# A^T h of a four-layer graph network in 64x64 parts of the TensorE array

## The chip, the cores and the metric

The kernel runs on one core of one Trainium2 chip. The metric is the device time of one execution in microseconds (us), lower is better. A core has TensorE (PE in the profile; its weight loads are listed apart as PEld), VectorE (DVE), ScalarE (ACT), GpSimd (POOL) and the engine that issues transfers (SP). Each engine takes its instructions from a queue of its own, in the order in which the program put them there. Matmuls write to PSUM, which has eight banks of 2 KB per partition; the other data live in SBUF.

## What is computed

128 graphs of 64 nodes with 256 features pass through four layers, each with a layer norm, a ReLU and a residual: attention with four heads, attention with one head, a relational layer, and a gated graph network with three GRU steps. The change concerns the last one:

```python
def _gru_cell(inp, h, w_ih, w_hh, b_ih, b_hh):
    gi = inp @ w_ih.T + b_ih
    gh = h @ w_hh.T + b_hh
    i_r, i_z, i_n = jnp.split(gi, 3, axis=-1)
    h_r, h_z, h_n = jnp.split(gh, 3, axis=-1)
    r = jax.nn.sigmoid(i_r + h_r)
    z = jax.nn.sigmoid(i_z + h_z)
    n = jnp.tanh(i_n + r * h_n)
    return (1.0 - z) * n + z * h

def _L3_gnn_ref(x, adj, weight, w_ih, w_hh, b_ih, b_hh):
    A = (adj != 0).astype(x.dtype)
    h = x
    for i in range(3):
        m = jnp.einsum('bnd,de->bne', h, weight[i])
        aggr = jnp.einsum('bst,bsd->btd', A, m)
        h = _gru_cell(aggr, h, w_ih, w_hh, b_ih, b_hh)
    return h

# each layer:
h = jnp.maximum(_layernorm(x, axis=-1), 0.0)
x = x + layer(h, adj, ...)
```

All data are fp32. The kernel uses A^T (h W) = (A^T h) W: it forms A^T h and multiplies it with the combined weights `wc` (weight[i] times w_ih).

## The kernel before

Two graphs lie side by side on the 128 partitions and make a pair; four pairs (G = 4, eight graphs, T = 512 columns) make a group, and there are 16 groups. The 256 features are two chunks of 128 (K = 2). The state h is kept with features on the partitions (`hT`) and, for A^T h, with nodes on the partitions (`hnat`); `abd` holds the adjacency as 0 and 1.

`along` forms one chunk c of A^T h for a group. A graph has only 64 nodes, so a product sums over 64 partitions. The two graphs of a pair stand on the two halves of the partitions, and their products use the two halves of the array's rows at the same time; each has 64x128 weights (`hnat`) and streams the 64 columns of `abd`. `beside` enters such a set of products into the plan as one operation of the given cost.

```python
def beside(products, cost):
    def emit():
        for product in products:
            nc.nc.tensor.matmul(*[real(x) for x in product], start=True, stop=True)
    ...
    nc.note("PE", emit, cost, ...)

def along(psum, hnat, abd, aT, c):
    pa, pb = psum.tile([P, G, N], F32, name="tp"), psum.tile([P, G, N], F32, name="tq")
    products = []
    for p in range(G):
        for half, ps in ((0, pa), (1, pb)):
            b = slice(half * N, (half + 1) * N)
            products.append((ps[:, p, :], hnat[b, p, c * P : (c + 1) * P], abd[b, p, :]))
    beside(products, 700.0)
    to = aT[:, c, :].rearrange("p (g a j) -> p a g j", a=2, j=N)
    nc.scalar.copy(to[:, 0], pa)
    nc.scalar.copy(to[:, 1], pb)
```

It is called for both chunks ahead of the recurrence, and for each chunk in steps 1 and 2 of the recurrence; step 0 takes the A^T h formed ahead of it.

```python
def before_recurrence(work, psum, src, adjacency, abd, by_dma=False):
    ... # layer norm: hT and hnat; abd
    for c in range(K):
        along(psum, hnat, abd, aT, c)
    ... # sums of parts of hT and aT

# recurrence, step i (gate, mul, both: matmuls with 128x128 weights):
a.gate("nh", 0)
if i > 0:
    aT = work.tile([P, K, T], F32, name="aT")
    along(psum, hnat, abd, aT, 0)
    state_sums(aT, aS, 0)
a.mul("ry", 1, 1)
a.m1_there()
a.gate("ni", 0)
if i > 0:
    back(hT, hnat, 1)          # transposes chunk 1 of the state into hnat
a.gate("nh", 1)
a.nh_there()
if i > 0:
    along(psum, hnat, abd, aT, 1)
    state_sums(aT, aS, 1)
...
```

The attention layers have a set in 64x64 parts already. The rows of the array are halved by r, its output columns by a, and each r has a PSUM bank of its own (`mm`, `mn`):

```python
for h in range(heads):
    for a in range(2):
        for r in range(2):
            b, s, to = slice(r * N, (r + 1) * N), 2 * u + a, slice(a * N, (a + 1) * N)
            products.append((pv[r][to, h, :], t[b, s * heads + h, :], wv[b, s, h, :]))
beside(products, 800.0 if heads > 1 else 600.0)
```

The program isn't emitted in the order in which it is written. A plan notes every operation with an estimated cost in ns, its dependencies and a stretch of time (a job with start and end), from which it gets a due time; it then simulates the engines and emits, on each engine, the operation that can start first, by due time among equals. `LATENCY` is what the simulation adds between an operation and its user on another engine. So costs, latency and stretches decide only the order in each queue. The recurrence of a group runs while the first three layers of later groups fill the gaps.

```python
LATENCY = 176.7
...
nc.begin("weights", 18.0, 84.9)
...
start, period = 94.8, 82.2
...
at = start + g * period
nc.begin(("before", g), at - (13.0 if g == 0 else 17.8), at, ...)
before(g)
nc.begin(("recur", g), at, at + period)
recur(g)
```

Of the kernel before, what the change touches and what calls it, by code (L numbers as in the profile page):

```python
# [8 lines left out]
F32 = mybir.dt.float32  # L9
# [7 lines left out]
P = 128  # L17
N = 64
D = 256
K = D // P  # L20
G = 4
# [115 lines left out]
class Pool:  # L137
# [3 lines left out]
    psum = False  # L141
# [66 lines left out]
class Plan:  # L208

    LATENCY = 176.7

    def __init__(self, nc):
        self.nc, self.on, self.ops, self.job = nc, False, [], None
# [221 lines left out]
def kernel(  # L437
# [28 lines left out]
    nc = Plan(tc.nc)  # L466
# [128 lines left out]
# [8 lines that stand above are left out]
        if not nc.on:  # L603
            return emit()
        writes = list({id(x[0].base): x[0] for x in products}.values())
        nc.note("PE", emit, cost, [Plan.all_of(x) for x in writes], [x for p in products for x in p[1:]])
# [57 lines left out]
    def aggregate_graphs(work, psum, t, wv, heads):  # L664


        fo = D // heads
        n = wv.shape[1]
        o = work.tile([P, n, heads, fo], F32, name="o")
        for u in range(n // 2):  # L670
            banks = [psum.tile([P, 512], F32, name=name) for name in ("mm", "mn")]
            pv = [po[:, : D + heads].rearrange("p (h f) -> p h f", h=heads) for po in banks]
# [3 lines that stand above are left out]
                    for r in range(2):  # L676
                        b, s, to = slice(r * N, (r + 1) * N), 2 * u + a, slice(a * N, (a + 1) * N)
                        products.append((pv[r][to, h, :], t[b, s * heads + h, :], wv[b, s, h, :]))
            beside(products, 800.0 if heads > 1 else 600.0)
            for r in range(2):  # L680
                rec = work.tile([P, heads], F32, name="rec")
                nc.vector.reciprocal(rec, pv[r][:, :, fo])
                nc.vector.tensor_tensor(
                    o[:, 2 * u + r], pv[r][:, :, :fo], rec[:, :, None].to_broadcast([P, heads, fo]), ALU.mult
                )
        return o.rearrange("p g h f -> p g (h f)")

    def along(psum, hnat, abd, aT, c):

        pa, pb = psum.tile([P, G, N], F32, name="tp"), psum.tile([P, G, N], F32, name="tq")  # L690
        products = []
        for p in range(G):
            for half, ps in ((0, pa), (1, pb)):
                b = slice(half * N, (half + 1) * N)
                products.append((ps[:, p, :], hnat[b, p, c * P : (c + 1) * P], abd[b, p, :]))
        beside(products, 700.0)
        to = aT[:, c, :].rearrange("p (g a j) -> p a g j", a=2, j=N)
        nc.scalar.copy(to[:, 0], pa)
        nc.scalar.copy(to[:, 1], pb)
        return 0.9  # L700

# [23 lines left out]
    def before_recurrence(work, psum, src, adjacency, abd, by_dma=False):  # L727

        hT = work.tile([P, K, T], F32, name="hT")
        hnat = work.tile([P, G, D], F32, name="hnat")  # L730
        if by_dma:
            layernorm_T_by_dma(work, src, hT, hnat)
        else:
            layernorm_T(work, psum, src, hT, natural=hnat)
        nc.vector.tensor_scalar(abd, adjacency, 0.0, None, op0=ALU.not_equal)
        aT = work.tile([P, K, T], F32, name="aT")
        for c in range(K):
            along(psum, hnat, abd, aT, c)
        hS = work.tile([P, 4, T // 2], F32, name="hS")
        aS = work.tile([P, 4, T // 2], F32, name="aS")  # L740
        for k in range(K):
            state_sums(hT, hS, k)
            state_sums(aT, aS, k)
        return hT, aT, hS, aS

    def recurrence(work, psum, start, src, abd, store):

        hT, aT, hS, aS = start
# [102 lines left out]
        for i in range(LAYERS):  # L851
            last = i == LAYERS - 1
            hnew = work.tile([P, K, T], F32, name="hT")
            a = Chunk(0, i, hT, hnew)

            a.mul("ry", 1, 0)
            a.gate("nh", 0)
            if i > 0:
                aT = work.tile([P, K, T], F32, name="aT")
                along(psum, hnat, abd, aT, 0)  # L860
                state_sums(aT, aS, 0)
            a.mul("ry", 1, 1)
            a.m1_there()
            a.gate("ni", 0)
            if i > 0:
                back(hT, hnat, 1)
            a.gate("nh", 1)
            a.nh_there()
            if i > 0:
                along(psum, hnat, abd, aT, 1)  # L870
                state_sums(aT, aS, 1)
            a.mul("rm", 2, 0) + a.mul("rz", 7, 0)
            a.mul("rm", 2, 1)
            a.r_there(S0)
            a.mul("rz", 7, 1)
            a.gate("ni", 1)
            a.n_there(S0)
            a.both("ry", 6)
            a.m16_there()
            b = Chunk(1, i, hT, hnew)  # L880
            b.both("rm", 2)
            a.both("ry", 5)
            a.m165_there()
            a.z_there(S1)
            b.gate("nh", 0)
            a.both("ry", 3)
            a.r_there(S1)
            a.n_there(S1)
            a.h_there(S1)
            a.both("rz", 4)  # L890
            a.z_there(S0)
            a.h_there(S0)

            b.gate("nh", 1)
            b.nh_there()
            b.both("ry", 1)
            b.m1_there()
            b.r_there(S0)
            b.both("rz", 7)
            b.both("ry", 6)  # L900
            b.m16_there()
            b.gate("ni", 0)
            b.both("ry", 5)
            b.m165_there()
            b.z_there(S1)
            hnat = work.tile([P, G, D], F32, name="hnat")
            back(hnew, hnat, 0, src if last else None)
            b.both("ry", 3)
            b.r_there(S1)
            b.gate("ni", 1)  # L910
            b.n_there(S0)
            b.n_there(S1)
            b.h_there(S1)
            b.both("rz", 4)
            b.z_there(S0)
            b.h_there(S0)
            hT = hnew
            if not last:
                for k in range(K):
                    state_sums(hT, hS, k)  # L920
# [5 lines left out]
    with ExitStack() as s1:  # L926
# [34 lines left out]
        psum = Banks(s1.enter_context(tc.tile_pool(name="psum", bufs=1, space=PSUM)), 1, Banks.own)  # L961
# [203 lines left out]
        def loop_relation(g, p0, n, pool):  # L1165

            src = XG[g][:, p0 : p0 + n]
            hT = pool.tile([P, K, n * P], F32, name="hT")
# [16 lines left out]
            products = []  # L1185
            for u in range(n // 2):
                for a in range(2):
                    for r in range(2):
                        b, s = slice(r * N, (r + 1) * N), 2 * u + a
                        products.append((po[r][a * N : (a + 1) * N, u, :], oh[b, s, :], v[b, s, :]))  # L1190
            beside(products, 1050.0 * n / 4)
            for r in range(2):
                to = src.rearrange("p (u r) d -> p r u d", r=2)[:, r]
                nc.vector.scalar_tensor_tensor(to, po[r], 0.0, to, op0=ALU.max, op1=ALU.add)
# [34 lines left out]

        nc.begin("columns")  # L1230
        first_weights()
        nc.begin("weights", 18.0, 84.9)
        later_weights(early)
        layers = (first_layer, second_layer, third_layer)
        start, period = 94.8, 82.2
        users = {}
        for g in range(NG):
            if g > 1:
                load_group(g)

            if g == 0:
                units = [(0, 2, (-3.0, 30.1, 57.3, 72.2)), (2, 2, (4.1, 32.9, 59.6, 78.0))]
            elif g == 1:
                units = [(0, 2, (28.7, 55.8, 87.9, 107.3)), (2, 2, (46.0, 70.1, 100.9, 126.4))]
            elif g == 2:
                units = [(0, G, (74.9, 112.9, 175.1, 237.8))]
            else:
                end = start + g * period - 28.8
                units = [(0, G, [end - 52.1 * i for i in (3, 2, 1, 0)])]
            for p0, n, at in units:  # L1250
                spare = g == 0 and p0 > 0
                for i in range(3):
                    nc.begin((g, p0, i), at[i], at[i + 1], [users[i]] if i in users and not spare else [])
                    if not spare:
                        users[i] = (g, p0, i)
                    layers[i](g, p0, n, spare)
            if g == 0:
                nc.begin("make")
                nc.note("-", make_gru, 0.0, [], [], [op for op in nc.ops if any(b.pool is early for b in op.bases)])
            at = start + g * period  # L1260
            nc.begin(("before", g), at - (13.0 if g == 0 else 17.8), at, [("recur", g - 2)] if g > 1 else [])
            before(g)
            nc.begin(("recur", g), at, at + period)
            recur(g)
# [240 lines left out]
```

## Time and profile before

| | before |
|---|---|
| device time, median of 3 (us) | 1477.09 (1475.32 to 1477.32) |
| profiled span (us) | 1473.8 |
| granted TensorE clock, mean | 0.991 |
| sets of A^T h | 96, each of 8 products, 16 records |
| weight load of A^T h, median (ns) | 188 |
| weight load of attention, 64x64, median (ns) | 133 |
| copy of A^T h out of PSUM, 128x256, median (ns) | 372 |

In the groups of instructions, `tp<-abd,hnat 64*128 64x64 f32` is a matmul that writes the tile `tp` and reads `abd` and `hnat`, with weights of 64 rows and 128 columns, and an output as long as 64 columns. The duration of one record holds the passage through the array, and records overlap; what an operation costs the queue is read from the starts of successive records. An fp32 product is two records.

### The profile page before, as it was taken

Reading aid. Unit: us, or ns where it says so; the run is one execution under the profiler, and the core shown is the slowest. Engines: PE = TensorE matmul, PEld = TensorE weight load, DVE = VectorE, ACT = ScalarE, POOL = GpSimd, SP = SyncE. Lnnn points to the kernel's source line nnn. Section 1 sums busy time; section 2 is a strip of 40 time slices with the busy share of each in tenths; the row PEclk is TensorE's granted clock in tenths of the full one; section 3 lists DMA queues with packets and bytes.
Section 4 is the critical chain, followed back from the end, with each engine's and each line's share of the span. In section 5 each row is a group of like instructions: output and inputs, shape, how many; then the busy total and the mean of one; then the engine's idle time right before and its main releaser. Section 6 shows DMA issues by size and latency. Waiting matters only on the chain.

```text
span 1473.8 us, 24378 instructions
## 1 busy us (share of the span) xinstructions
PE 1428.2 (97%) x7925; PEld 981.2 (67%) x7925; DVE 1034.8 (70%) x2743; ACT 783.8 (53%) x1885; POOL 597.3 (41%) x744
## 2 busy tenths in 40 slices
PE   4989999999999999999999999999999999999996
PEld 3556776767667676766767676676767667666764
DVE  6678486785857778586776858577786968765543
ACT  3655556455555645555555555555555565544543
POOL 2424433444534444452434344344434434352432
PEclk8999999999999999999999999999999999999998
DMA  7011122212222121222212222221212122110000
GB/s 207 18 27 28 31 59 37 69 28 41 61 50 63 33 59 40 44 62 49 64 31 51 49 46 62 45 68 26 45 38 45 44 42 57 23 32 16 15 15 18
DMA packets 298863, 67.67 MB, mean 46 GB/s; under 512 B 274664, under 2 KB 296936, under 8 KB 298728
## 3 DMA queue, kind: packets, MB, share of 16 engines
q1 hardware_dynamic: 298168, 65.50, 21.3%
q8 instruction: 66, 1.08, 0.3%
q10 hardware_dynamic: 560, 0.52, 0.2%
q14 instruction: 69, 0.57, 0.1%
HBM read 28.06 MB, written 8.53 MB: 25 GB/s over the span
## 4 chain that ended last, share of the span: by engine, by line
PE 90%; DVE 5%; DMA 1%; SPq 1%; ACT 1%; issue 1%; POOL 0%; DVEq 0%
PE ry L380 22%; PE mm L380 15%; PE rz L380 11%; PE nh L380 11%; PE ni L380 11%; PE tp L601 6%; PE rm L380 6%; PE tp L380 4%; PE mm L601 3%; SPq L380 1%; DVE t L380 1%; DVE st L380 1%; DVE d L380 1%; DMA ihn<-in_L_gnn_w_ih_dram 1%; DMA hhn<-in_L_gnn_w_hh_dram 1%
## 5 line engine op out<-in xcount | busy, mean ns | idle before, releaser
L380 POOL TENSOR_TENSOR d<-hT,t 128x256 f32<-128x256 f32 x192 | 145.1, 763 | 492.9 <-ACT t L380 492.4
L380 PE MATMUL ni<-aT,wc 128*128 128x512 f32 x384 | 198.0, 599 | 0.2
L380 PE MATMUL nh<-hT,whh 128*128 128x512 f32 x384 | 194.7, 596 | 0.0
L380 DVE SCALAR_TENSOR_TENSOR t<-r,t 128x256 f32<-128x256 f32 x192 | 111.3, 583 | 62.6 <-ACT r L380 53.7
L380 ACT ACTIVATE z<-z,brz 128x256 f32<-128x256 f32 x192 | 97.0, 505 | 101.4 <-DVE z L380 100.9
L380 ACT COPY z<-ry 128x256 f32<-128x256 f32 x192 | 70.9, 369 | 134.3 <-PE ry L380 100.0
L380 POOL TENSOR_TENSOR hS<-hT 128x256 f32<-128x256 f32 x96 | 74.8, 783 | 136.0 <-PE ry L380 97.1
L380 DVE SCALAR_TENSOR_TENSOR d<-z,d 128x256 f32<-128x256 f32 x192 | 102.8, 545 | 36.7 <-POOL d L380 22.9
L601 PEld LDWEIGHTS tp<-abd,hnat 64*128 64x128 f32 x768 | 92.6, 187 | 48.8 <-issue 11.0
L380 PE MATMUL rz<-hS,whh 128*128 128x256 f32 x384 | 117.7, 388 | 2.4 <-DVE z L380 2.4
L380 ACT ACTIVATE hn<-xg,var,rstd 128x256 f32<-128x256 f32 x200 | 107.5, 594 | 20.4 <-DVE var L380 19.3
L380 PE MATMUL ry<-hS,wsum 128*128 128x256 f32 x384 | 116.7, 386 | 0.9 <-ACT z L380 0.8
L380 PE MATMUL mm<-wl,hT 128*128 128x512 f32 x248 | 116.2, 598 | 0.0
L380 PE MATMUL ry<-aS,wsum 128*128 128x256 f32 x384 | 114.2, 379 | 0.0
L380 PE MATMUL rz<-aS,wc 128*128 128x256 f32 x384 | 114.2, 379 | 0.0
L380 DVE TENSOR_TENSOR z<-rz,z 128x256 f32<-128x256 f32 x192 | 80.3, 418 | 47.5 <-PE rz L380 27.6
L380 ACT ACTIVATE t<-t,bi 128x256 f32<-128x256 f32 x192 | 94.9, 503 | 31.9 <-DVE t L380 30.9
L601 PE MATMUL tp<-abd,hnat 64*128 64x64 f32 x768 | 105.8, 278 | 0.0
L601 PE MATMUL tq<-abd,hnat 64*128 64x64 f32 x768 | 105.8, 278 | 0.0
L380 PEld LDWEIGHTS ry<-hS,wsum 128*128 128x128 f32 x384 | 70.1, 190 | 46.8 <-issue 24.8
L380 DVE SCALAR_TENSOR_TENSOR hT<-d,t 128x256 f32<-128x256 f32 x192 | 95.4, 510 | 4.2 <-DVE d L380 0.5
L380 POOL TENSOR_TENSOR aS<-aT,aS 128x256 f32<-128x256 f32 x96 | 75.9, 791 | 54.9 <-ACT aT L380 54.9
(200 smaller groups left out, 3270.2 us busy)
## 6 DMA issues: line engine op xcount, KB each, us to landing
hT<-hn SPq DMA_DIRECT2D x896, 32.0 KB, 1.9
out_dram<-hnat SPq DMA_DIRECT2D x16, 512.0 KB, 3.4
xg<-in_x_dram SPq DMA_DIRECT2D x15, 512.0 KB, 4.8
t<-row SPq DMA_DIRECT2D x28, 256.0 KB, 4.2
at<-in_adj_dram SPq DMA_DIRECT2D x64, 32.0 KB, 2.2
eg<-in_adj_dram SPq DMA_DIRECT2D x64, 32.0 KB, 2.2
ag<-in_adj_dram SPq DMA_DIRECT2D x16, 128.0 KB, 2.4
t<-row SPq DMA_DIRECT2D x28, 64.0 KB, 2.8
```

What stands on the lines that cost most here:

```text
L380: return do(*[real(a) for a in args], **{k: real(v) for k, v in kwargs.items()})
L601: nc.nc.tensor.matmul(*[real(x) for x in product], start=True, stop=True)
```

## The change

Three things are changed.

1. `along` now forms its products in 64x64 parts: the 128 features of a chunk are split in two halves f, which go to the two halves of the array's columns. With the two graphs of a pair on the two halves of its rows, four products can stand side by side. There are twice as many products, each with 64x64 weights.
2. `along` takes a list of chunks. Ahead of the recurrence both chunks are formed in one set, with one PSUM bank for each row half and one copy out of each bank. Within the recurrence the chunks stay apart; a branch for merging them there is switched off (`if 0`).
3. The plan's costs of the sets, its latency and its stretches are given new values. That changes the order in the queues, and no operation.

The first two are for less time of TensorE on A^T h; the third is for an order that fits.

```diff
-    LATENCY = 176.7
+    LATENCY = 160.9
@@ aggregate_graphs
-            beside(products, 800.0 if heads > 1 else 600.0)
+            beside(products, 710.0 if heads > 1 else 660.0)
@@
-    def along(psum, hnat, abd, aT, c):
-
-        pa, pb = psum.tile([P, G, N], F32, name="tp"), psum.tile([P, G, N], F32, name="tq")
+    def along(psum, hnat, abd, aT, cs):
+
+        banks = [psum.tile([P, len(cs), G, N], F32, name=name) for name in ("tp", "tq")]
         products = []
-        for p in range(G):
-            for half, ps in ((0, pa), (1, pb)):
-                b = slice(half * N, (half + 1) * N)
-                products.append((ps[:, p, :], hnat[b, p, c * P : (c + 1) * P], abd[b, p, :]))
-        beside(products, 700.0)
-        to = aT[:, c, :].rearrange("p (g a j) -> p a g j", a=2, j=N)
-        nc.scalar.copy(to[:, 0], pa)
-        nc.scalar.copy(to[:, 1], pb)
+        for i, c in enumerate(cs):
+            for p in range(G):
+                for half, ps in enumerate(banks):
+                    b = slice(half * N, (half + 1) * N)
+                    for f in range(0, P, N):
+                        products.append((ps[f : f + N, i, p, :], hnat[b, p, c * P + f : c * P + f + N], abd[b, p, :]))
+        beside(products, 230.0 + 480.0 * len(cs))
+        to = aT[:, cs[0] : cs[-1] + 1, :].rearrange("p c (g a j) -> p a c g j", a=2, j=N)
+        for half, ps in enumerate(banks):
+            nc.scalar.copy(to[:, half], ps)
@@ before_recurrence
-        for c in range(K):
-            along(psum, hnat, abd, aT, c)
+        along(psum, hnat, abd, aT, range(K))
@@ recurrence
-                along(psum, hnat, abd, aT, 0)
+                if 0:
+                    back(hT, hnat, 1)
+                    along(psum, hnat, abd, aT, range(K))
+                else:
+                    along(psum, hnat, abd, aT, [0])
...
-                along(psum, hnat, abd, aT, 1)
+                if not 0:
+                    along(psum, hnat, abd, aT, [1])
@@ loop_relation
-            beside(products, 1050.0 * n / 4)
+            beside(products, 230.0 + 216.0 * n)
@@ the plan's stretches
-        nc.begin("weights", 18.0, 84.9)
+        nc.begin("weights", 18.0, 79.1)
-        start, period = 94.8, 82.2
+        start, period = 99.2, 83.2
-                units = [(0, 2, (-3.0, 30.1, 57.3, 72.2)), (2, 2, (4.1, 32.9, 59.6, 78.0))]
+                units = [(0, 2, (0.2, 24.7, 61.4, 71.1)), (2, 2, (-0.6, 32.2, 60.6, 75.0))]
... # the units of groups 1 and 2 likewise
-                end = start + g * period - 28.8
-                units = [(0, G, [end - 52.1 * i for i in (3, 2, 1, 0)])]
+                end = start + g * period - 26.2
+                units = [(0, G, [end - 55.6 * i for i in (3, 2, 1, 0)])]
-            nc.begin(("before", g), at - (13.0 if g == 0 else 17.8), at, ...)
+            nc.begin(("before", g), at - (13.0 if g == 0 else 21.2), at, ...)
```

More of the change, by code (lines that the diff above doesn't have):

```diff
@@ L686, in aggregate_graphs @@
         return o.rearrange("p g h f -> p g (h f)")
-    def along(psum, hnat, abd, aT, c):
-        pa, pb = psum.tile([P, G, N], F32, name="tp"), psum.tile([P, G, N], F32, name="tq")
+    def along(psum, hnat, abd, aT, cs):
+        banks = [psum.tile([P, len(cs), G, N], F32, name=name) for name in ("tp", "tq")]
         products = []
-        for p in range(G):
-            for half, ps in ((0, pa), (1, pb)):
-                b = slice(half * N, (half + 1) * N)
-                products.append((ps[:, p, :], hnat[b, p, c * P : (c + 1) * P], abd[b, p, :]))
-        beside(products, 700.0)
-        to = aT[:, c, :].rearrange("p (g a j) -> p a g j", a=2, j=N)
-        nc.scalar.copy(to[:, 0], pa)
-        nc.scalar.copy(to[:, 1], pb)
-        return 0.9
+        for i, c in enumerate(cs):
[8 more added lines that the diff above has]
+            nc.scalar.copy(to[:, half], ps)
     def weight_sums(w, ws):
@@ L864, in recurrence @@
             a.gate("ni", 0)
-            if i > 0:
+            if i > 0 and not 0:
                 back(hT, hnat, 1)
@@ L1241 @@
             if g == 0:
-                units = [(0, 2, (-3.0, 30.1, 57.3, 72.2)), (2, 2, (4.1, 32.9, 59.6, 78.0))]
+                units = [(0, 2, (0.2, 24.7, 61.4, 71.1)), (2, 2, (-0.6, 32.2, 60.6, 75.0))]
             elif g == 1:
-                units = [(0, 2, (28.7, 55.8, 87.9, 107.3)), (2, 2, (46.0, 70.1, 100.9, 126.4))]
+                units = [(0, 2, (27.2, 56.6, 87.4, 98.1)), (2, 2, (44.7, 71.4, 101.8, 129.4))]
             elif g == 2:
-                units = [(0, G, (74.9, 112.9, 175.1, 237.8))]
+                units = [(0, G, (72.8, 120.6, 177.5, 238.7))]
             else:
-                end = start + g * period - 28.8
-                units = [(0, G, [end - 52.1 * i for i in (3, 2, 1, 0)])]
+                end = start + g * period - 26.2
+                units = [(0, G, [end - 55.6 * i for i in (3, 2, 1, 0)])]
             for p0, n, at in units:
@@ L1260 @@
             at = start + g * period
-            nc.begin(("before", g), at - (13.0 if g == 0 else 17.8), at, [("recur", g - 2)] if g > 1 else [])
+            nc.begin(("before", g), at - (13.0 if g == 0 else 21.2), at, [("recur", g - 2)] if g > 1 else [])
             before(g)
```

## The prediction

> **What bounds the kernel now.** I first read the page's busy times.
>
> ```profile
> span 1473.8 us, 24378 instructions
> PE 1428.2 (97%) x7925; PEld 981.2 (67%) x7925; DVE 1034.8 (70%) x2743; ACT 783.8 (53%) x1885; POOL 597.3 (41%) x744
> ```
>
> TensorE (PE) is busy 97% of the span and the next engine 70%. A busy PE can still be badly used, because matmuls are pipelined, so I asked next for the busy time by stretches, to see where the missing 3% lies.
>
> ```profile
> 0.00:100.00 100.00, 74.67 (x422) 46.49 (x422) 68.85 (x228) 51.23 (x137) 33.13 (x55) 0.91 0.35 90
> ...
> 800.00:1000.00 200.00, 198.92 (x1143) 137.72 (x1142) 146.71 (x393) 109.37 (x262) 82.19 (x100) 1.00 0.25 54
> 1400.00:1474.00 74.00, 60.66 (x280) 41.41 (x278) 29.32 (x66) 29.56 (x68) 20.91 (x28) 0.94 0.05 16
> ```
>
> The columns after the length are PE, weight loads, DVE, ACT and POOL. PE idles for 25 us in the first 100 and for 13 us in the last 74; between them it is over 99% busy, at full clock. So for about 1300 us the time is the sum of what PE has queued: work taken from PE there comes off the span one for one, as long as the order of the queue keeps every wait hidden.
>
> The third view is the timeline of PE around one set of A^T h, to see what such a set costs the queue, and not what its records add up to.
>
> ```profile
> 703.39 0.59 PE L380 MATMUL rz<-aS,wc 128*128 128x256 f32 x2
> 703.92 0.32 PE L601 MATMUL tp<-abd,hnat 64*128 64x64 f32 x1
> ...
> 704.08 0.27 PE L601 MATMUL tp<-abd,hnat 64*128 64x64 f32 x1
> ...
> 704.19 0.27 PE L601 MATMUL tp<-abd,hnat 64*128 64x64 f32 x1
> ...
> 704.75 0.27 PE L601 MATMUL tq<-abd,hnat 64*128 64x64 f32 x1
> 704.95 0.49 PE L380 MATMUL mm<-w0e,hT 128*128 128x264 f32 x1
> ```
>
> Every fp32 product is two records here. Two records of 256 columns before the set take 0.43 us from start to start (702.96 to 703.39), 0.84 ns a column and record. They have therefore streamed by 703.82, the set begins at 703.92, and the next full-array matmul at 704.95: the set holds the queue for **1.13 us**. Worked out in this way from the starts of the matmuls, all 96 sets of the trace have a median of 1.131 us. Within the set, a pair of records starts every 0.11 us (704.08, 704.19). Streaming 64 columns would take 54 ns; loading 128 columns of weights at the same 0.84 ns takes 107 ns. So the load of 128 columns sets the pace, not the 64 columns that stream.
>
> The kernel already has a set in the form that the change uses, the 16 products of the four-headed attention:
>
> ```profile
> 726.18 0.59 PE L380 MATMUL ry<-aT,wc 128*128 128x256 f32 x2
> 726.71 0.27 PE L601 MATMUL mm<-wh,t 64*64 64x65 f32 x1
> ...
> 726.87 0.22 PE L601 MATMUL mm<-wh,t 64*64 64x65 f32 x1
> ...
> 726.93 0.22 PE L601 MATMUL mm<-wh,t 64*64 64x65 f32 x1
> ...
> 727.19 0.22 PE L601 MATMUL mn<-wh,t 64*64 64x65 f32 x1
> 727.38 0.67 PE L380 MATMUL rz<-hS,whh 128*128 128x256 f32 x2
> ```
>
> Here four records start together and the next four come 57 ns later (726.87, 726.93). The preceding product has streamed by 726.61, so the set holds the queue 0.77 us; the median of its 29 undisturbed sets is **0.719 us**. It has twice the records of a set of A^T h and takes 0.41 us less.
>
> **What the Trainium skill says.** "TensorE: Matmul & The Clock Gate", Part 2 (Step-by-step), says that a weight load's time goes with its column count and not with its rows; the paces of 107 and 57 ns for 128 and 64 weight columns agree. The same page (Part 1, the passage on 56 and 53.3 ns) gives a floor of about 25 ns from start to start of matmuls however small; the trace does not agree for side-by-side parts, four starts in 57 ns being 14 ns each, so I apply no such floor. "TensorEngine Tiling (Array Packing)", Tiling Modes (Key Properties), says that a change of tiling mode drains TensorE; the trace agrees, with 0.09 us of lead into each set and a first matmul after it of 0.50 us for two records in place of 0.43 (727.38 to 727.88). Its Performance Considerations (PSUM Bottleneck) warns that evacuation can become the bound behind packed parts; ACT, which evacuates here, is 53% busy, so I expect no bound there.
>
> **The change part by part.**
>
> *A set of one chunk* (four for each group, in GRU steps 1 and 2; 64 in all, since their merging is switched off by the "if 0"). 8 products become 16, with 64 weight columns in place of 128. The cost is that of the attention set with 64 streamed columns instead of 65: 0.719 less 8 times 0.84 ns, about 0.712 us. It saves 1.131 - 0.712 = 0.42 us, times 64 = **26.8 us**.
>
> *The set ahead of the recurrence* (one for each group, 16 in all). Two sets of 1.131 us become one with 32 products: 0.712 plus eight more rounds of 57 ns, 1.17 us. It saves 2.262 - 1.17 = 1.09 us, times 16 = **17.5 us**. One entry and exit of the tiling mode falls away too; the entry is in the 1.131, the slower restart afterwards (0.07 to 0.1 us) is not: 16 times 0.09 = **1.4 us**. ACT evacuates with two copies of 512 columns (an aT-like copy of 512 takes 585 ns median, one of 256 takes 372) instead of four of 256, 0.3 us less per group, off the path. The first chunk becomes available later, ahead of the recurrence, where other matmuls are at hand.
>
> The sum is 45.7 us of PE time, 2.86 us a group. About one set in ten lies in the filling or in the tail, where PE isn't the bound. In the tail the sets stand in the dependent chain itself and a shorter set shortens it, so I count 95%: 43 us.
>
> *The plan.* The constants for attention (800 to 710, 600 to 660) and the relation (1050 to 1094 for four pairs, 525 to 662 for two) move no work; they alter only the order in which operations enter the queues. The old plan took a set of A^T h at 700 ns against 1131 measured, the new one takes 710 against my 712. So the old PE was always later than planned, 2.6 us a group, and everyone else had that as a cushion. The new plan loses the cushion and also takes a smaller allowance for the hand-over between engines (160.9 in place of 176.7 ns). Some waits should surface. At present, gaps over 150 ns on PE outside the sets come to 9 us between 110 and 1390 us; I allow 0.3 us a group more, 5 us. The later start of the first recurrence in the plan (94.8 to 99.2) and the earlier end of the weights (84.9 to 79.1) can shift the filling by a few us either way: I put nothing.
>
> 1477.1 - 43 + 5 = 1439; since the constants look newly matched to the shorter sets, I take **1437 us**, a ratio of 0.973. As a check, the relation's matmuls in the chain of waits recur at 1006.72, 1092.87 and 1179.01 us, a period of 86.1; less 2.86 that is 83.3, close to the new plan's 83.2.
>
> **The rivals.**
>
> 1. *The parts don't run side by side.* The attention set starts its products with alternating row halves; the new set has two column parts of the same row half in succession, then the other. If the queue can't overlap a load and a matmul of one row half, a set stays at 107 ns or more for each four records: 8 rounds of 107 and 0.27, 1.13 us, as before, and only the merging saves, 16 times some 0.35: 1471 us. Against it: four starts within 20 ns in the attention set already include pairs of the same row half. I give it 8%.
> 2. *PE stops being the bound.* If the GRU's chain through ACT, DVE and POOL sets the period, PE would show gaps. DVE's 1035 us are 72% of 1437, so no engine fills up; it would be latency, in a plan with less cushion. At 1 us a group given back, this makes 1450.
> 3. *The new stretches cost at the ends.* Everything before the recurrence of group 0 waits for loads and weights. A start later by the plan's 4.4 us would make 1441; a better filling might make 1432.
> 4. *Shorter than worked out.* If the sets overlap their neighbours better, or the plan recovers some of the 38 us idle at the ends, 1425.
>
> **Range and chances.** Rivals 2 and 3 make the upper side the wider one: 1425 to 1454 us. Faster by over 2% means below 1447.5, which needs two thirds of the PE saving: 0.80. Within 2% covers rival 1 and a bad case of rival 2: 0.18. Slower by over 2% would need a new order that goes badly wrong: 0.02.
>
> **What would show it.** Right: records of A^T h with 64x64 weights, 3072 in place of 1536, in rounds of four some 57 ns apart; a set of one chunk holding the queue 0.70 to 0.74 us, the double one 1.15 to 1.20; PE still over 98% busy between 200 and 1300 us; a period near 83.3. Wrong in the first step: single sets above 1 us. Wrong in the assumption that PE stays the bound: right set times, but idle PE in the middle, with waits for DVE, ACT or POOL ahead of the GRU's matmuls. Wrong about the plan: gains or losses that lie in the first 110 or the last 80 us.

## The result and the profile after

The changed kernel takes **1442.23 us** (median, 1441.65 to 1443.76) against 1476.81 for the kernel before in the same comparison, a ratio of 0.977 (95% interval 0.9752 to 0.9786). The predicted 1437 is 5 us too low.

The page of the changed kernel begins:

```profile
span 1440.1 us, 27350 instructions
PE 1387.4 (96%) x9461; PEld 942.8 (65%) x9461; DVE 1044.3 (73%) x2743; ACT 779.0 (54%) x1853; POOL 596.5 (41%) x744
```

PE has 1536 more matmul records and is busy 41 us less. The timeline of PE around a set of one chunk:

```profile
471.63 0.59 PE L380 MATMUL rz<-aS,wc 128*128 128x256 f32 x2
472.15 0.27 PE L601 MATMUL tp<-abd,hnat 64*64 64x64 f32 x2
...
472.32 0.23 PE L601 MATMUL tp<-abd,hnat 64*64 64x64 f32 x2
...
472.38 0.22 PE L601 MATMUL tp<-abd,hnat 64*64 64x64 f32 x2
...
472.62 0.23 PE L601 MATMUL tq<-abd,hnat 64*64 64x64 f32 x2
472.78 0.70 PE L380 MATMUL ry<-hT,whh 128*128 128x256 f32 x2
```

The weights are now 64*64, and each line stands for two records (x2), so a `tp` and a `tq` line are a round of four. A round starts every 0.06 us (472.32, 472.38). The product ahead has streamed by 472.06, the next full-array matmul starts at 472.78: 0.72 us, where the old set took 1.13.

Stretches of the kernel before, and then of the kernel after (columns: stretch, its length, then busy PE, weight loads, DVE, ACT, POOL, then clock and transfers):

```profile
100.00:400.00 300.00, 297.60 (x1722) 205.73 (x1722) 220.32 (x593) 163.48 (x392) 129.67 (x156) 1.00 0.22 44
400.00:700.00 300.00, 298.88 (x1653) 205.78 (x1653) 212.88 (x568) 164.16 (x395) 122.80 (x149) 1.00 0.25 49
700.00:1000.00 300.00, 298.17 (x1706) 207.45 (x1705) 220.81 (x579) 163.14 (x392) 127.60 (x154) 1.00 0.25 51
1000.00:1300.00 300.00, 299.98 (x1659) 207.20 (x1658) 223.04 (x576) 163.24 (x392) 121.81 (x153) 1.00 0.21 41
```

```profile
100.00:400.00 300.00, 294.47 (x2091) 199.75 (x2091) 228.48 (x599) 164.17 (x392) 128.91 (x158) 1.00 0.21 44
400.00:700.00 300.00, 299.36 (x2080) 206.01 (x2079) 227.94 (x592) 168.08 (x403) 131.34 (x161) 1.00 0.25 50
700.00:1000.00 300.00, 299.87 (x2058) 204.88 (x2057) 235.64 (x610) 167.82 (x395) 124.92 (x154) 1.00 0.25 53
1000.00:1300.00 300.00, 295.40 (x2045) 201.61 (x2044) 221.91 (x573) 164.29 (x390) 132.98 (x157) 1.00 0.21 42
```

Busy PE over these 1200 us falls from 1194.6 to 1189.1 us. In the two middle stretches the kernel after is the fuller one; it idles in the first and the last.

Such a table misses the small gaps between pipelined matmuls, so I made an account of PE's queue from the starts in the trace: a full-array matmul streams 0.842 ns a column and record; what passes beyond that until the next start is a gap; a gap over 125 ns counts as idle, and so does what a set waits beyond its usual lead or is followed by beyond the usual restart.

| us | before | after | difference |
|---|---|---|---|
| streaming of full-array matmuls | 1214.5 | 1214.5 | 0 |
| sets of A^T h | 108.8 | 66.1 | -42.7 |
| sets of attention and relation | 64.3 | 65.4 | +1.1 |
| restarts and gaps up to 125 ns | 26.0 | 25.4 | -0.6 |
| **idle** | 45.6 | 54.2 | **+8.6** |
| before the first and after the last matmul starts | 14.7 | 14.6 | -0.1 |
| span | 1473.9 | 1440.2 | -33.7 |

The sets give 43 us, and PE's idle time takes 9 of them back. The experiments ask why. What lengthened the sets of attention and relation by 1.1 us was not followed up.

### The profile page after: what moved, and what is told of

Read it like the earlier page. It is cut to its first block, busy times and chain, and to the rows that moved or that the text cites. A ratio compares the mean times of both kernels' runs of the same rounds, so it can differ in the third digit from the quotient of the medians.

```text
span 1440.1 us, 27350 instructions
## 1 busy us (share of the span) xinstructions
PE 1387.4 (96%) x9461; PEld 942.8 (65%) x9461; DVE 1044.3 (73%) x2743; ACT 779.0 (54%) x1853; POOL 596.5 (41%) x744
## 4 chain that ended last, share of the span: by engine, by line
PE 80%; DVE 7%; SPq 5%; ACT 3%; issue 2%; DMA 2%; POOL 1%; DVEq 0%; POOLq 0%; ACTq 0%
PE ry L380 21%; PE mm L380 15%; PE ni L380 10%; PE rz L380 10%; PE nh L380 10%; PE rm L380 5%; SPq L380 5%; PE tp L380 4%; PE mm L601 3%; PE tp L601 3%; DVE t L380 1%; ACT hn L380 1%; DVE d L380 1%; DMA t<-row 1%; DVE hn L380 1%
## 5 line engine op out<-in xcount | busy, mean ns | idle before, releaser
L380 POOL TENSOR_TENSOR d<-hT,t 128x256 f32<-128x256 f32 x192 | 149.7, 790 | 456.1 <-ACT t L380 454.2
L380 PE MATMUL ni<-aT,wc 128*128 128x512 f32 x384 | 195.1, 596 | 1.2 <-DVE t L380 1.2
L380 DVE SCALAR_TENSOR_TENSOR t<-r,t 128x256 f32<-128x256 f32 x192 | 107.3, 563 | 63.7 <-ACT r L380 53.2
L380 POOL TENSOR_TENSOR hS<-hT 128x256 f32<-128x256 f32 x96 | 78.3, 819 | 154.9 <-PE ry L380 124.8
L380 DVE SCALAR_TENSOR_TENSOR d<-z,d 128x256 f32<-128x256 f32 x192 | 109.6, 580 | 29.1 <-POOL d L380 19.0
L380 POOL TENSOR_TENSOR rstd<-var,mhalf 128x4 f32<-128x4 f32 (+1 forms) x70 | 68.2, 975 | 75.4 <-DVE var L380 73.8
L380 DVE BATCH_NORM_STATS2 st<-xg 128x6 f32<-128x256 f32 x256 | 96.6, 411 | 3.0 <-DMA xg<-in_x_dram 3.0
L380 POOL TENSOR_TENSOR hS<-hT,hS 128x256 f32<-128x256 f32 x96 | 73.4, 765 | 46.3 <-DVE hT L380 44.2
L380 PEld LDWEIGHTS ni<-aT,wc 128*128 128x128 f32 x384 | 71.6, 190 | 24.1 <-issue 10.6
```

The costliest lines, as they stand in the source:

```text
L380: return do(*[real(a) for a in args], **{k: real(v) for k, v in kwargs.items()})
```

## The experiments

The theories: **cushion**, the one of the prediction (the old plan took the sets for 0.43 us shorter than they were, which left every other engine ahead of PE; true costs take that slack away); **stretches** or **allowance** (the new stretches or the smaller latency cost idle time by themselves); **fit** (an order is fitted by all values of the plan together to one set of products, and any pair that doesn't belong together idles). All idle times below are from the same account.

### Products and plan exchanged

`new_products_old_plan`: the kernel after with the latency, the weights' stretch, start, period and all units of before:

```diff
-    LATENCY = 160.9
+    LATENCY = 176.7
-        nc.begin("weights", 18.0, 79.1)
+        nc.begin("weights", 18.0, 84.9)
-        start, period = 99.2, 83.2
+        start, period = 94.8, 82.2
... # all units and offsets likewise
```

The costs of all sets stay at the new values, those of attention and relation too, so this plan differs from that of before in these costs. They were not moved alone.

> The products of the kernel after (64x64 parts, merged ahead of the recurrence, with their new costs) in the plan of before (latency 176.7, all stretches as before). Sets of A^T h hold the queue 0.72 and 1.19 to 1.25 us in each case. Theory 'cushion' (PE's idle time grew by 9 us because the shorter sets leave no slack in any plan): PE idle again about 54 us, 1440 to 1445 us. Rival 'stretches' (it grew because of the new latency and stretches): PE idle about 45 us as before, 1432 to 1436 us. If the old stretches no longer fit the shorter sets, so that the new stretches were needed for the gain: over 1448 us.

Measured: 1452.48 us, ratio to before 0.984 (0.982 to 0.985). The sets total 65.6 us, as after; idle is 60.4 us, and the restarts and small gaps rise to 30.7.

`old_products_new_plan`: the kernel before with all the opposite edits, and the new costs of the attention and relation sets; its own sets stay planned at 700.

> The products of the kernel before (64x128 parts, one set per chunk, cost 700) in the plan of after (latency 160.9, all new stretches, new costs of the attention and relation sets). Theory 'cushion': the sets are 0.41 us longer than planned again, the slack is back, PE idle about 45 us, 1474 to 1479 us. Rival 'stretches': the new plan costs 9 us by itself, 1484 to 1488 us. If the new plan brings part of the gain: below 1470 us.

Measured: 1486.90 us, ratio 1.006 (1.0046 to 1.008). The sets total 109.6 us, idle is 55.6. Its stretches:

```profile
100.00:400.00 300.00, 293.51 (x1686) 202.17 (x1684) 216.97 (x563) 160.54 (x386) 121.78 (x147) 1.00 0.21 44
...
1000.00:1300.00 300.00, 297.36 (x1635) 205.53 (x1634) 221.48 (x577) 162.15 (x384) 123.17 (x149) 1.00 0.21 40
```

What follows is read from the four together:

| | plan of before | plan of after |
|---|---|---|
| products of before | 1477 us, idle 46 | 1487 us, idle 56 |
| products of after | 1452 us, idle 60 | 1442 us, idle 54 |

In the plan of after, the products alone bring 44.7 us, nearly the 45.7 worked out for PE's time in the prediction. In the plan of before they bring 24.5. The new plan costs 10 us with the old products and gains 10 with the new ones. "Cushion" falls: the slack of understated sets is there in `old_products_new_plan`, and it idles 56 us. "Stretches" alone falls too, because the old ones idle still more with the new products. Of the 44.7 us, 43.5 are the sets; in the plan of before the sets give as much, and some 19 us of it go back into idle time and small gaps.

### One value of the plan moved

`latency_176`: the kernel after with one line changed.

```diff
-    LATENCY = 160.9
+    LATENCY = 176.7
```

> The kernel after with the plan's latency at 176.7 in place of 160.9; all stretches, costs and products as after. Theory 'allowance' (the smaller latency lets more waits surface): PE idle falls from 54 us toward 46, 1434 to 1439 us. Rival 'fit' (the order is fitted by all values of the plan together, and any of them moved alone makes it worse): PE idle over 58 us, 1446 to 1465 us, with the same sets of A^T h.

Measured: 1467.19 us, ratio to before 0.992 (0.9907 to 0.9942); sets 65.9 us, idle 78.0. A larger allowance made it 25 us slower. Its stretches show that the idle time is spread through the middle:

```profile
100.00:400.00 300.00, 290.84 (x2045) 196.94 (x2044) 217.41 (x570) 159.14 (x382) 126.30 (x153) 0.99 0.21 44
400.00:700.00 300.00, 292.42 (x1981) 198.01 (x1980) 223.72 (x581) 164.06 (x390) 128.44 (x153) 0.99 0.24 48
```

The other engines are no busier in these two stretches than in the kernel after; PE's queue has its matmuls in another order, and stands at some of them.

`cost_understated`:

```diff
-        beside(products, 230.0 + 480.0 * len(cs))
+        beside(products, 280.0 if len(cs) == 1 else 390.0)
```

> The kernel after, with the plan's cost of a set of A^T h understated by as much as the old one was (280 for one chunk, 390 for two, against 0.72 and 1.25 us on the chip); products and all else as after. Theory 'cushion' (an understated set leaves every other engine slack): PE idle falls toward 46 us, 1433 to 1438 us. Rival 'fit': no gain from it, 1443 to 1455 us.

Measured: 1463.96 us, ratio 0.9905 (0.9888 to 0.9921), idle 76.0. This is the direct test of "cushion": the kernel is 22 us slower than the kernel after, where "cushion" has it 4 to 9 us faster.

`old_true_cost`: the kernel before with

```diff
-        beside(products, 700.0)
+        beside(products, 1131.0)
```

> The kernel before with the cost of a set of A^T h in the plan at the 1131 ns that the trace shows, in place of 700; nothing else changed. If truer costs by themselves make a better order, 1468 to 1475 us. Theory 'fit' (the stretches and the latency were fitted with the false cost in place): 1480 to 1500 us, all of the difference PE idle time, with the sets at 1.131 us as before.

Measured: 1513.44 us, ratio 1.024 (1.022 to 1.026), sets 109.5 us, idle 78.4, even above the expected range. A truer cost alone is no better order.

### Merging less, and more

`not_merged`: the kernel after, with a set for each chunk ahead of the recurrence.

```diff
-        along(psum, hnat, abd, aT, range(K))
+        for c in range(K):
+            along(psum, hnat, abd, aT, [c])
```

> The kernel after, but with one set for each chunk ahead of the recurrence too, in 64x64 parts. Two sets of 0.718 us in place of one of 1.19 to 1.25 us, and one more restart of 0.09 us: by PE's sum alone 16 times about 0.3 us, 4 to 5 us more, 1446 to 1448 us. If a change of order outweighs it, the time lies off this by some us to either side, and PE's idle time shows it.

Measured: 1448.75 us (1446.76 to 1451.10). The sets are at 69.8 us (3.7 more than after), restarts 0.6 more, idle 54.4. So merging is worth about 4 us of PE's time, of the 6.5 by which the medians of the two kernels, timed in different comparisons, differ.

`merged_everywhere`: the switched-off branch switched on, in all its three conditions.

```diff
-                if 0:
+                if 1:
                     back(hT, hnat, 1)
                     along(psum, hnat, abd, aT, range(K))
...
-            if i > 0 and not 0:
+            if i > 0 and not 1:
                 back(hT, hnat, 1)
...
-                if not 0:
+                if not 1:
                     along(psum, hnat, abd, aT, [1])
```

> The kernel after with the switched-off branch switched on: in GRU steps 1 and 2 too, both chunks of A^T h are formed in one set, after the transposes of both chunks of the state. By PE's sum: 32 sets fewer entries and exits, 2 times 0.718 plus 0.09 less 1.19 to 1.25, about 0.3 us each, 9 us less: 1433 us, if PE stays the bound. Rival: the first chunk now waits for the second chunk of the state, which comes last, so PE gets gaps of over 0.4 us ahead of these sets or behind them: PE idle over 75 us, 1450 to 1475 us.

Measured: 1494.95 us, ratio 1.011 (1.009 to 1.013). The sets fall to 59.0 us, 7.1 less, and idle rises to 114.6. The waits of this kernel (columns: who waited for whom, us in total, times, longest):

```profile
PE rm L380 <- DVE hT L380: 17.1, 9, 3.1
PE ry L380 <- ACT z L380: 14.8, 14, 2.0
```

`hT` is the new state, which DVE writes last in a step. In the kernel after, no wait of PE for `hT` ahead of `rm` is among its seven largest. The reading is that, with everything of A^T h behind both chunks of the state, PE has too little ahead of it to do; it is argued from these waits, 32 of the 115 us of idle time. The order was not fitted anew for this kernel, so part of the loss may be that.

### What sets the pace of a set

`stream_128`: the kernel before, each product streaming its adjacency twice; the second copy is left unused.

```diff
-        pa, pb = psum.tile([P, G, N], F32, name="tp"), psum.tile([P, G, N], F32, name="tq")
+        pa, pb = psum.tile([P, G, 2, N], F32, name="tp"), psum.tile([P, G, 2, N], F32, name="tq")
-                products.append((ps[:, p, :], hnat[...], abd[b, p, :]))
+                products.append((ps[:, p], hnat[...], abd[b, p, None, :].to_broadcast([N, 2, N])))
... # the copies take the first of the two
```

> The kernel before, with each product of A^T h streaming its 64 columns of the adjacency twice (128 columns, the second copy is not used); weights stay 64x128. Theory 'the weight load of 128 columns sets the pace': pairs still start every 0.107 us, a set holds the queue 1.13 to 1.19 us, the time is within 6 us of the kernel before. Rival 'load and stream follow one another within a part' (54 ns of each): pairs every 0.16 us, a set of 1.56 us, about 1518 us.

Measured: 1481.0 us in one run. The timeline of PE around a set:

```profile
706.38 0.59 PE L380 MATMUL rz<-aS,wc 128*128 128x256 f32 x2
706.90 0.37 PE L601 MATMUL tp<-abd,hnat 64*128 64x128 f32 x1
...
707.11 0.27 PE L601 MATMUL tp<-abd,hnat 64*128 64x128 f32 x1
...
707.23 0.27 PE L601 MATMUL tp<-abd,hnat 64*128 64x128 f32 x1
...
707.79 0.27 PE L601 MATMUL tq<-abd,hnat 64*128 64x128 f32 x1
707.99 1.16 PE L380 MATMUL mm<-w0e,hT 128*128 128x264 f32 x4
```

Twice the streaming, and from the second pair on, pairs still start every 0.112 us, as in the kernel before (mean of six steps in both). The set's median is 1.184 us, 0.053 longer. All of that lies between the first pair and the second: 0.213 us here (706.90 to 707.11), 0.160 in the kernel before (703.92 to 704.08); from the last pair to the matmul behind the set it is 0.202 us in both. 64 more columns stream for 0.054 us at 0.842 ns each, so the streaming counts in the first step, as the rival has it, and in no later one. There the pace goes with the 128 columns of weights, as the prediction has it. The records of the weight loads fit this: 188 ns for 128 columns in the kernel before, 135 for 64 in the kernel after, 0.83 ns for each column of difference.

`alternating`: the kernel after with the row half as the innermost loop in place of the column half.

```diff
-                for half, ps in enumerate(banks):
-                    b = slice(half * N, (half + 1) * N)
-                    for f in range(0, P, N):
+                for f in range(0, P, N):
+                    for half, ps in enumerate(banks):
+                        b = slice(half * N, (half + 1) * N)
```

> The kernel after with the products of a set in the order of the attention's set: the row half alternates fastest and the column half more slowly. The plan and so the order of all other operations are the same. If the order within a round of four matters, the sets of one chunk leave 0.718 us (by over 0.05); if not, they stay within 0.01 of it and the time within 3 us of the kernel after (1442 us).

Measured: 1444.52 us in one run. The sets of one chunk have a median of 0.718 us again, of two chunks 1.253. The order within a round doesn't matter to what a set costs.

### A plan fitted to the new products

If "fit" holds, better values must exist. They were sought with the plan's own simulation, which counts the true set costs since the change: small random moves of the stretches, each kept when the simulated end came earlier. Products, costs and latency stay as after. `refit_a`:

```diff
-        nc.begin("weights", 18.0, 79.1)
+        nc.begin("weights", 18.0, 77.4)
-        start, period = 99.2, 83.2
+        start, period = 99.2, 83.3
-   (0, 2, (0.2, 24.7, 61.4, 71.1)), (2, 2, (-0.6, 32.2, 60.6, 75.0))
+   (0, 2, (0.2, 24.7, 57.7, 72.6)), (2, 2, (-0.6, 32.2, 63.5, 75.0))
-   (0, 2, (27.2, 56.6, 87.4, 98.1)), (2, 2, (44.7, 71.4, 101.8, 129.4))
+   (0, 2, (27.2, 58.1, 87.4, 98.1)), (2, 2, (44.7, 71.2, 98.1, 129.4))
-   (0, G, (72.8, 120.6, 177.5, 238.7))
+   (0, G, (72.8, 120.6, 177.5, 238.2))
-                end = start + g * period - 26.2
-                units = [(0, G, [end - 55.6 * i for i in (3, 2, 1, 0)])]
+                end = start + g * period - 27.8
+                units = [(0, G, [end - 57.0 * i for i in (3, 2, 1, 0)])]
-  at - (13.0 if g == 0 else 21.2)
+  at - (13.0 if g == 0 else 15.1)
```

> The kernel after with only its stretches changed (all products, costs and the latency as after), to those for which the plan's own simulation ends earliest, at 1402 us where it says 1437 for the kernel after. If the fit of the order is what holds the rest of the time (theory 'fit'), PE idle falls below the 54 us of the kernel after, and the time below 1438 us; about 1430 us is what is left if the idle time between 110 and 1360 us goes and the ends stay. If the plan's simulation doesn't rank orders as the chip does: 1440 us or more, with idle PE in the middle.

Measured: **1427.65 us** (1426.61 to 1427.78), ratio to before 0.966 (0.9651 to 0.9677). Its stretches:

```profile
100.00:400.00 300.00, 298.04 (x2110) 203.91 (x2109) 228.12 (x606) 169.89 (x402) 132.57 (x160) 1.00 0.22 45
400.00:700.00 300.00, 299.24 (x2089) 208.79 (x2088) 220.22 (x600) 170.08 (x404) 130.42 (x160) 1.00 0.25 51
700.00:1000.00 300.00, 299.80 (x2095) 207.08 (x2094) 228.95 (x615) 170.61 (x402) 128.03 (x157) 1.00 0.25 52
1000.00:1300.00 300.00, 298.30 (x2074) 205.09 (x2076) 219.14 (x568) 166.27 (x388) 128.56 (x158) 1.00 0.21 42
```

Against the kernel after, the first and last stretch are filled: idle is 43.8 us, 10.4 less, restarts and small gaps 22.6, 2.8 less, and the sets 65.0, 1.1 less. Of what idles, 28.6 us lie in the first 110 us, as in the kernel after (28.5).

`refit_b` and `refit_c` are other ends of such searches: the first recurrence due at 100.6 and at 93.0 among their edits (`refit_c` changes besides it the weights to 82.6, two times of group 0 and the later units' offset to 30.5).

> As refit_a with other stretches, for which the plan's simulation ends at 1415 us, with the first recurrence later (100.6). Same two readings: below 1438 us if its ranking holds, 1440 us or more if it doesn't.

> As refit_a with four changes alone: the first recurrence due at 93.0 in place of 99.2, the weights at 82.6 in place of 79.1, the first layers of the second half of group 0 moved by some us, the offset of the later units 30.5 in place of 26.2; the plan's simulation ends at 1419 us. Below 1438 us if its ranking holds, 1440 us or more if it doesn't.

Measured: 1433.73 us (ratio 0.971, 0.9692 to 0.9722; idle 48.9) and 1438.75 us (0.9745, 0.973 to 0.976; idle 50.3). The simulated ends of the three, 1402, 1415 and 1419, rank as the chip does, though the chip's spread is smaller.

The simulation is part of every kernel's program, and its end can be read for the other orders too. Where the sets of A^T h have their true costs:

| us | after | not_merged | new_products_old_plan | latency_176 | merged_everywhere | old_true_cost |
|---|---|---|---|---|---|---|
| simulated end | 1437 | 1435 | 1443 | 1457 | 1473 | 1495 |
| device time | 1442 | 1449 | 1452 | 1467 | 1495 | 1513 |

With the three refits these are nine orders, and the simulation ranks them as the chip does, but for `not_merged` and the kernel after. The chip is 5 to 25 us later. With untrue costs the simulation is 34 to 51 us too early and ranks badly: 1443 for the kernel before (1477), 1436 for `old_products_new_plan` (1487), 1427 for `cost_understated` (1464). So the loss of `latency_176` is no whim of the chip: the plan itself counts this order as 20 us worse, though some of that may be the larger latency that it counts with.

`refit_a` also bears on "cushion" and "allowance": it has neither understated sets nor the larger latency, and idles 43.8 us, less than the 45.6 of the kernel before, which had both.

## Why the prediction was right, and where it was not

**PE is the bound, and a set's time comes off one for one.** Right for PE's sum: streaming is the same to 0.1 us, and in the plan of after the new products took 44.7 us off. The condition that the prediction set, an order that keeps every wait hidden, is the weak part: in the plan of before the same products took off 24.5. Of the rivals, the second came true in part, with idle PE in the middle, and the third hardly (1.4 us in the first 110 us).

**A set of one chunk, 0.712 us.** It is 0.718 (median of 64), a saving of 26.4 us where 26.8 was worked out. That the attention set could stand in for it was right, with its order of products (`alternating`) not mattering; the first rival is out.

**The set of two chunks, 1.17 us.** The term is somewhat too small: a round takes 58.3 ns (mean of the steps after the first) where 57 was read from two lines, and 0.718 plus eight such rounds is 1.185. That is what it measures where nothing follows late, and at least 1.254 in the eleven of 16 that are followed by the attention's matmul `mm<-w0e`. All 16 in `refit_a`, none followed by that matmul, take 1.185 to 1.190. What holds those 70 ns was not tried; it is not that matmul as such, for in `new_products_old_plan` a set ahead of it takes 1.184. Both kinds of set together saved 42.7 us where 44.3 had been worked out, and the restarts 0.6 where 1.4 was.

**45.7 taken at 95%, 43 us.** The account has 43.3 for sets and restarts, and that it agrees is luck: the 5% were meant for sets in the filling and the tail, and what is missing is the size of the double sets and of the restarts.

**"I allow 0.3 us a group more, 5 us."** This is the step that failed, in size and in cause. Idle time rose by 8.6 us: 1.4 in the first 110 us, and the rest in the middle, in the first and last of the four stretches shown, ahead of matmuls that wait for ACT or DVE. Two such waits of the kernel after:

```profile
PE ry L380 <- ACT z L380: 3.5, 5, 1.2
PE mm L601 <- DVE t L380: 3.2, 3, 1.5
```

All of the first and 1.8 us of the second lie between 110 and 1360 us; in the kernel before, the same stretch has 0.8 us of the first and none of the second. The causes given were a lost cushion and the smaller allowance between engines. Putting either back made the kernel slower (`cost_understated` 1464 us, `latency_176` 1467 us), and `refit_a` idles less than the kernel before without either. What the runs showed in its place is fit: moving one value of the plan cost 22 to 37 us, and the exchange of products and plan cost 10 on either side of the table. Why the fitted order of the kernel after stands at just these matmuls stays open.

**1439 taken down to 1437, "since the constants look newly matched".** The new constants do belong to the new products (10 us better there than the old ones), but they were no optimum: other stretches found 14.6 us more by the medians of the two kernels. The reason was half right and the 2 us had nothing to stand on. By the spans the gain is 33.7 us where 40.1 was predicted. The difference is 3.6 us of idle time beyond the 5 allowed, the 1.1 us of attention and relation and these 2 us, less 0.3 us by which sets and restarts gave more than 43.

**The period near 83.3.** In the chain of waits of the kernel after, the relation's matmuls recur so:

```profile
397.75 3.63 PE mm L380 x8
...
480.98 3.63 PE mm L380 x8
...
564.22 3.63 PE mm L380 x8
```

That is 83.2 us, as predicted from the sum of PE's work. It holds from about 360 to 1110 us; just ahead of that stretch and behind it, where PE idles, the sets ahead of the recurrence start some 86 us apart.

## What to carry to other kernels

When a set of small products runs slower than its columns stream, compare the pace of its starts with the time that its weight columns take to load: splitting the weights over more parts of the array can pay although every column streams just as long. Where a program's order comes from a plan, a gain in one operation may be only half delivered until the plan is fitted again: here the same products were worth 24.5 us in the old plan and 44.7 in the new one, and the next fit added 15. And making one constant of a plan true doesn't by itself make the order better. It makes the plan's own simulation usable for a new search of the values that were fitted around it; the order is then judged on the chip.

## What the runs showed of the hardware

In parts with 128 weight columns, pairs start every 0.112 us whether 64 columns stream (the kernel before) or 128 (`stream_128`); only from the first pair to the second is it 0.160 and 0.213 us. Four parts of 64x64 take a round every 58 ns, four records each (the kernel after). A set pays about 0.09 us of lead and, after it, 0.07 to 0.1 us in a first full-array matmul of 256 columns or more, in the kernel before with its 64x128 parts and in the kernel after with its 64x64 parts alike.
